# Cross-attention in two layers: an output projection and a later unit's query projection share one slot, and K and V are made in halves in the slots between

## The chip, the cores and the metric

The kernel runs on one core of one Trainium2 chip. Its time is the device time in microseconds (us) of one execution. The median of three runs of the kernel before is 974.39 us (973.72 to 974.40).

The engines by their short names: PE is TensorE (matmuls), and PEld its weight loads; DVE is VectorE; ACT is ScalarE; POOL is GpSimd; SP is SyncE, which only issues DMAs here.

## What is computed

Two cross-attention layers in a row over x, 32 samples of 256 positions by 320 channels, all in fp32. Each sample has a context of 77 rows by 512 channels, the same in both layers. Per layer, with 20 heads of 16 channels:

```python
q = heads(x @ Wq);  k = heads(ctx @ Wk);  v = heads(ctx @ Wv)
p = softmax(q @ k.T / 4)               # over the 77 context rows
x = merge(p @ v) @ Wo + bias + x
```

The reference has more branches (object, "others" and image keys), but the context has exactly the 77 text rows, so the other branches get no rows.

## The kernel before

**Units.** Samples go in 16 pairs. A unit is one pair in one layer, so there are 32 units. Four pairs of layer 0 come first, and then layer 1 of a pair and layer 0 of a later one alternate. Channels lie on the partitions: channels 0 to 255 as two blocks of 128 rows (each 2 samples x 256 columns), and the last 64 channels of both samples together as one block of 128 rows, sample 0 above sample 1 (columns `2*NT:NX`). A *group* g is one such 128 x 256 piece; g = 0 to 3 are the main pieces (channel block g//2, sample g%2), g = 4 is the block of last channels.

**Work of a unit.** Keys and values are projected from the context (`keys`, `keys_rest`, `vals`), queries from x (`queries` for groups 0 to 3, `queries_rest` for group 4). `maxima` computes scores with queries as rows, and DVE takes each row's maximum. `turn` transposes these on DVE, and eight small DMAs write them into spare rows of q. Keys are kept in two masked forms: `kT` for `maxima` (`mask_keys`, POOL) and `kM` for `scores` (`less_keys`, POOL). `scores` computes scores with keys as rows, now less the maximum, and ACT takes the exponentials. `values` multiplies them with V (`products`), then DVE transposes the result (`turned`), takes the reciprocal of the sums, and POOL multiplies (`normal`). `turn_back` transposes it back on DVE into `oT`. `finish` and `finish_rest` are the output projection for groups 0 to 3 and for group 4; `add` (DVE) adds bias and x. `store` writes x out after layer 1. V is made by chunks of 128 context rows, 20 chunks a layer, over the limits of pairs (`load_chunk`, `vals`), and then copied by DMA to the unit that needs it (`place_vals`).

**Tiles on PE.** Every projection is cut into column tiles of 32 output channels (`by_columns`, line 183). A product over 320 input channels has two full steps over 128 rows (`main_channels`) and one over the last 64. For groups 0 to 3 the last 64 channels are taken as 64-row tiles, sample 0 in rows 0 to 63 and sample 1 in rows 64 to 127, in different PSUM banks (`last_channels`, line 196). For group 4 (`project_rest`, line 217) all three steps have 128 rows; the third uses a weight `w22` that is block-diagonal, so that half of its rows are zeros. A matmul in fp32 shows as two records in the profile. Maxima and scores use 32-row tiles.

**PSUM.** One pool of eight banks serves everything; a bank is handed out again in turn, once its reader is done.

**Order.** The program is written in slots, by hand (lines 490 to 569). Unit u begins its scores at slot s = 5u, and there are five slots a unit, each with one group of maxima (of the next unit but one, or the next), one of scores, one of values, and some projection as filler. Within a slot the kinds of work come in the order of line 565: load, maxima, turn, scores, values, rest, back, full, last. `at(slot, where, step)` puts a step in its place. Each engine and each DMA queue then runs its own instructions in this order. Relative to s, before: x loads at s-14, context at s-12, `queries` at s-9 ("last"), `keys` at s-8, `keys_rest` at s-7, `vals` at s-6 (and s-5, where a second chunk is needed), `queries_rest` and `less_keys` at s-5, maxima from s-6 to s-2, `turn` at s-2, scores from s, values and `turn_back` one slot after each, `finish` at s+6 ("full"), `finish_rest` at s+8. So `finish` of one unit and `queries` of the third next stand in the same slot. The last units but one (`late`) have their output projections in parts, over the slots at the end, which have no other filler.

Of the kernel before, what the change touches and what calls it, by code (L numbers as in the profile page):

```python
# [47 lines left out]
F32 = mybir.dt.float32  # L49
# [6 lines left out]
P = 128  # L56
NB = 2
# [33 lines left out]
def xattn_kernel(ctx: ExitStack, tc: tile.TileContext, xT, cT, cP, weights, outT):  # L91
# [104 lines left out]
    def last_channels(ps, w2, x, ts=(0, 1), **flags):  # L196
        for t in ts:
            for b in range(NB):
# [18 lines left out]
    def project_rest(ps, w, w22, x):  # L217

        for kc in range(3):
            for i in range(4):  # L220
                b, m = i // 2, i % 2
                r = slice(32 * i, 32 * i + 32)
                if kc < 2:
                    lhsT = w[:, kc, 2 * P + 32 * m : 2 * P + 32 * m + 32]
                    rhs = x[:, kc * NT + b * S : kc * NT + (b + 1) * S]
                else:
                    lhsT, rhs = w22[:, 0, r], x[:, 2 * NT : NX]
                nc.tensor.matmul(ps[r, 0:S], lhsT, rhs, start=(kc == 0), stop=(kc == 2))  # L228


    def mask_keys(u, g0, g1):

        kR, kT = st[u]["kr"], st[u]["k"]
        engine = nc.gpsimd if u else nc.vector
        for e in range(2):
            engine.tensor_scalar_mul(kT[:, e, g0:g1], kR[:, g0:g1], masks[:, e : e + 1])  # L236
# [10 lines left out]
    def keys(u):  # L247
        p, layer = units[u]
        w, c_sb = w_sb[layer], cs[u]
        kR = st[u]["kr"] = work.tile([P, NG, L], F32, tag="kR", name=f"kR_{u}", bufs=2)  # L250
        st[u]["k"] = work.tile([P, 2, NG, L], F32, tag="kT", name=f"kT_{u}", bufs=3)
        for t in range(2):
            ps = bank(f"psk_{u}_{t}")
            for kc in range(NKA):
                by_columns(
                    ps[:, 0 : 2 * L],
                    w["k"][:, kc, t * P : (t + 1) * P],
                    c_sb[:, kc, :],
                    start=(kc == 0),
                    stop=(kc == NKA - 1),  # L260
                )
            nc.scalar.copy(kR[:, 2 * t : 2 * t + 2].rearrange("p g k -> p (g k)"), ps[:, 0 : 2 * L])  # L262
        mask_keys(u, 0, 4)

    def keys_rest(u):
# [4 lines left out]
        for kc in range(NKA):  # L270
            for i in range(4):
                b, m = i // 2, i % 2
# [8 lines left out]
        mask_keys(u, 4, 5)  # L281

    def queries(u):
        p, layer = units[u]
        w = w_sb[layer]
        q0, _ = st[u]["q"] = [
            work.tile([P, NX], F32, tag=f"q{e}", name=f"q{e}_{u}", bufs=3) for e in range(2)
# [377 lines left out]
```

## Time and profile before

| | |
|---|---|
| median of 3 runs | 974.39 us (973.72 to 974.40) |
| profiled execution, its own time | 974.26 us |
| its span, first to last instruction | 972.5 us |
| granted PE clock | 1.000 |
| PE busy | 965.8 us (99%) |
| DVE, ACT, POOL busy | 567.6 (58%), 430.2 (44%), 238.8 us (25%) |
| one unit in the middle (454.0 to 483.3 us) | 29.3 us |
| its longest slot (481.95 to 493.48: outputs and queries) | 11.53 us |
| its shortest slot (507.38 to 511.30: query rest) | 3.92 us |
| DMA, mean | 86 GB/s |

How to read the lines below. The page's first line gives, for each engine, busy time, share of the span and number of instructions. The chain is the work that ended last, followed back, as shares of the span. A line of waits reads: engine, tile and line, what it waited for, us in total, times, longest. A line of the timeline reads: start in us from the span's begin, length in us, engine, line, operation, output and inputs by tile, tile shape (rows*columns), operand shapes, number of instructions merged; in brackets the idle time before and what ended it. Ends of matmuls are modelled, so the distance from one group's start to the next's is the time that a group took.

### The profile page before, as it was taken

Reading aid. Unit: us, or ns where it says so; the run is one execution under the profiler, and the core shown is the slowest. Engines: PE = TensorE matmul, PEld = TensorE weight load, DVE = VectorE, ACT = ScalarE, POOL = GpSimd, SP = SyncE. Lnnn points to the kernel's source line nnn. Section 1 sums busy time; section 2 is a strip of 40 time slices with the busy share of each in tenths; the row PEclk is TensorE's granted clock in tenths of the full one; section 3 lists DMA queues with packets and bytes.
Section 4 is the critical chain, followed back from the end, with each engine's and each line's share of the span. In section 5 each row is a group of like instructions: output and inputs, shape, how many; then the busy total and the mean of one; then the engine's idle time right before and its main releaser. Section 6 shows DMA issues by size and latency. Waiting matters only on the chain.

```text
span 972.5 us, 43974 instructions
## 1 busy us (share of the span) xinstructions
PE 965.8 (99%) x19674; PEld 597.1 (61%) x19674; DVE 567.6 (58%) x1320; ACT 430.2 (44%) x937; POOL 238.8 (25%) x360
## 2 busy tenths in 40 slices
PE   8999999999999999999999999999999999999998
PEld 5666666666666666665666656666666666566654
DVE  2456555665655665556655556655566555565664
ACT  1445434454444454444544444544445444444543
POOL 2233221332221322212222223222132221232211
PEclk9999999999999999999999999999999999999999
DMA  6632122231132411223112232221322212230112
GB/s 221 238 103 79 46 71 97 71 100 46 55 124 72 135 47 59 97 82 124 56 60 87 70 126 72 73 73 65 126 82 71 69 52 98 71 107 25 49 58 83
DMA packets 54526, 83.60 MB, mean 86 GB/s; under 512 B 15620, under 2 KB 36228, under 8 KB 54338
## 3 DMA queue, kind: packets, MB, share of 16 engines
q1 hardware_dynamic: 53386, 78.29, 24.3%
q8 instruction: 154, 2.52, 1.1%
q10 hardware_dynamic: 952, 2.50, 0.7%
q14 instruction: 34, 0.28, 0.1%
HBM read 35.39 MB, written 10.49 MB: 47 GB/s over the span
## 4 chain that ended last, share of the span: by engine, by line
PE 99%; DVE 1%; POOL 0%; issue 0%; ACT 0%; POOLq 0%
PE po L412 16%; PE psq L186 15%; PE psy L186 15%; PE pss L392 14%; PE psm L357 12%; PE psv L186 9%; PE psk L186 7%; PE psq L228 4%; PE psy L228 4%; PE psk L273 2%; PE warm L179 0%; DVE max L365 0%; DVE kT L236 0%; POOL stage L156 0%; POOL normal L433 0%
## 5 line engine op out<-in xcount | busy, mean ns | idle before, releaser
L398 ACT ACTIVATE pT<-pss 77x512 f32<-77x512 f32 x640 | 327.4, 591 | 209.0 <-PE pss L392 209.0
L365 DVE TENSOR_REDUCE max<-psm 128x4 f32<-128x308 f32 x640 | 260.4, 469 | 179.2 <-PE psm L357 175.5
L433 POOL TENSOR_TENSOR normal<-turned,inv 128x256 f32<-128x256 f32 x160 | 99.5, 622 | 677.6 <-DVE inv L428 677.6
L412 PE MATMUL po<-pT,v 77*32 77x256 f32 x2560 | 171.5, 385 | 0.5 <-DVE max L365 0.5
L392 PE MATMUL pss<-q,kM 32*77 32x256 f32 x2560 | 168.6, 374 | 0.0
L186 PE MATMUL psq<-x,w 128*32 128x256 f32 (+1 forms) x3072 | 150.7, 382 | 0.0
L186 PE MATMUL psy<-oT,w 128*32 128x256 f32 (+1 forms) x3072 | 150.4, 380 | 0.0
L298 ACT COPY q<-psq 128x256 f32<-128x256 f32 x128 | 47.1, 373 | 204.0 <-PE psq L186 195.6
L424 DVE STREAM_TRANSPOSE turned<-po 128x512 f32<-128x512 f32 x160 | 113.4, 709 | 39.0 <-PE po L412 36.0
L447 DVE STREAM_TRANSPOSE oT<-normal 128x256 f32<-128x256 f32 x160 | 71.3, 445 | 108.4 <-POOL normal L433 108.4
L357 PE MATMUL psm<-kT,q 32*128 32x154 f32 x2560 | 129.0, 314 | 0.9 <-DVE kT L236 0.7
L357 PEld LDWEIGHTS psm<-kT,q 32*128 32x128 f32 x2560 | 92.1, 183 | 56.1 <-issue 34.6
L186 PEld LDWEIGHTS psq<-x,w 128*32 128x32 f32 (+1 forms) x3072 | 85.6, 109 | 58.7 <-issue 15.3
L412 PEld LDWEIGHTS po<-pT,v 77*32 77x32 f32 x2560 | 67.0, 109 | 87.8 <-DVE max L365 57.8
L186 PEld LDWEIGHTS psy<-oT,w 128*32 128x32 f32 (+1 forms) x3072 | 81.2, 108 | 63.4 <-issue 15.6
L392 PEld LDWEIGHTS pss<-q,kM 32*77 32x77 f32 x2560 | 102.2, 141 | 17.6 <-issue 1.2
L236 POOL TENSOR_SCALAR kT<-kR,masks 128x308 f32<-128x308 f32 (+1 forms) x124 | 93.9, 769 | 38.6 <-ACT kR L262 32.0
L454 DVE SCALAR_TENSOR_TENSOR x<-psy,w,x 128x256 f32<-128x256 f32 x160 | 68.6, 477 | 56.4 <-PE psy L186 51.3
L186 PE MATMUL psv<-w,cv 128*32 128x320 f32 x1232 | 93.5, 432 | 0.0
L186 PE MATMUL psk<-c,w 128*32 128x154 f32 x2048 | 73.2, 294 | 0.0
L186 PEld LDWEIGHTS psk<-c,w 128*32 128x32 f32 x2048 | 66.0, 110 | 6.7 <-issue 0.4
L186 PEld LDWEIGHTS psv<-w,cv 128*32 128x32 f32 x1232 | 41.1, 110 | 40.6 <-issue 2.2
(28 smaller groups left out, 354.0 us busy)
## 6 DMA issues: line engine op xcount, KB each, us to landing
q<-q SPq DMA_DIRECT2D x32, 640.0 KB
c<-in_cP_dram SPq DMA_DIRECT2D x32, 308.0 KB
cv<-in_cT_dram SPq DMA_DIRECT2D x38, 256.0 KB
out_dram<-x SPq DMA_DIRECT2D x15, 640.0 KB
x<-in_xT_dram SPq DMA_DIRECT2D x14, 640.0 KB
v<-stage SPq DMA_DIRECT2D x26, 192.5 KB
q<-mT SPq DMA_DIRECT2D x254, 5.0 KB
w<-in_w_dram ACTq DMA_DIRECT2D x2, 640.0 KB
```

The costliest lines, as they stand in the source:

```text
L186: nc.tensor.matmul(out[m : m + 32], lhsT[:, m : m + 32], rhs, **flags)
L228: nc.tensor.matmul(ps[r, 0:S], lhsT, rhs, start=(kc == 0), stop=(kc == 2))
L236: engine.tensor_scalar_mul(kT[:, e, g0:g1], kR[:, g0:g1], masks[:, e : e + 1])
L357: nc.tensor.matmul(ps[j][:, c * 2 * L : (c + 1) * 2 * L], q[r, c * P : (c + 1) * P], kT[r, :, g, :], start=True, stop=True,)
L365: nc.vector.tensor_reduce(mx[:, 2 * g : 2 * g + 2, 2 * j : 2 * j + 2], ps[j][:, : 4 * L].rearrange("p (c e k) -> p c e k", e=2, k=L), AX.X ...
L392: nc.tensor.matmul(ps[j][:L, e * S : (e + 1) * S], kM[r, e, g, :], q[r, :], start=True, stop=True,)
L398: nc.scalar.activation(st[u]["p", g][j][:L], ps[j][:L], AF.Exp, scale=SCALE)
L412: nc.tensor.matmul(po[32 * j : 32 * j + 32, e * S : (e + 1) * S], vpad[:L, b, pair, e].rearrange("p a d -> p (a d)"), pT[j][:L, e * S : (e ...
L424: nc.vector.transpose(turned[:, 0 : 2 * S], po)
L433: nc.gpsimd.tensor_tensor(normal.rearrange("p q e d -> p e q d"), outs, inv.unsqueeze(3).broadcast_to([P, 2, S // 32, HD]), ALU.mult,)
L447: nc.vector.transpose(of_group(st[u]["o"], g), normal)
L454: nc.vector.scalar_tensor_tensor(x, ps[:, 0:S], w_sb[layer]["b"][:, 0, t : t + 1], x, ALU.add, ALU.add)
```

## The change

- The output projection of unit u-3 and the query projection of unit u become one step, `outputs_and_queries`, at slot s-10, the rests of both included. It runs for units 3 to 30. Its order on PE: main channels of the outputs, main channels of the output rest, all last channels as 64-row tiles, main channels of the query rest, main channels of the queries. The last channels of the two rests no longer use the zero-padded 128-row step: each is cut by samples into 64-row tiles, and the query rest is laid out with the two samples swapped (`swap`), so that an output rest's tiles and a query rest's take different columns of the array. The layout of group 4 of keys and of the values' output follows that swap.
- That step opens ten PSUM banks: four and one for the outputs, one and four for the queries. The `add`s come behind all 64-row tiles.
- `keys` is made in two halves (slots s-9 and s-8), with `keys_rest` at s-9; `kT` becomes three tiles with a mask pass each. `vals` is made in two halves of 160 columns: at s-7 and s-6 for one new chunk, both halves of a chunk in a slot where there are two.
- Loads, maxima and `turn` come one slot earlier. `turn_back` of groups 0 to 3 moves to the next slot, behind its maxima ("turn back" in the order).
- The late units' parts are moved by one slot or more; `queries` and `queries_rest` stay separate for units 1, 2 and 31.

```diff
-    def last_channels(ps, w2, x, ts=(0, 1), **flags):
+    def last_channels(ps, w2, x, ts=(0, 1), bs=(0, 1), **flags):
...
-    def project_rest(ps, w, w22, x):
-        for kc in range(3):
+    def rest_tile(ps, i, lhsT, rhs, swap, **flags):
+        o = (32 * i + 64 * swap) % P
+        nc.tensor.matmul(ps[o : o + 32, 0:S], lhsT, rhs, **flags)
+    def rest_main(ps, w, x, start, stop, swap=0):
+        for kc in range(2):
             for i in range(4):
                 b, m = i // 2, i % 2
-                r = slice(32 * i, 32 * i + 32)
-                if kc < 2:
-                    lhsT = w[:, kc, 2 * P + 32 * m : 2 * P + 32 * m + 32]
-                    rhs = x[:, kc * NT + b * S : kc * NT + (b + 1) * S]
-                else:
-                    lhsT, rhs = w22[:, 0, r], x[:, 2 * NT : NX]
-                nc.tensor.matmul(ps[r, 0:S], lhsT, rhs, start=(kc == 0), stop=(kc == 2))
-    def mask_keys(u, g0, g1):
-        kR, kT = st[u]["kr"], st[u]["k"]
+                rest_tile(
+                    ps, i, w[:, kc, 2 * P + 32 * m : 2 * P + 32 * m + 32],
+                    x[:, kc * NT + b * S : kc * NT + (b + 1) * S], swap,
+                    start=(start and kc == 0), stop=(stop and kc == 1),
+                )
+    def rest_last(ps, w22, x, b, swap=0, **flags):
+        r = slice(64 * b, 64 * b + 64)
+        for i in (2 * b, 2 * b + 1):
+            rest_tile(ps, i, w22[r, 0, 32 * i : 32 * i + 32], x[r, 2 * NT : NX], swap, **flags)
...
+    def project_rest(ps, w, w22, x, swap=0):
+        rest_main(ps, w, x, start=True, stop=False, swap=swap)
+        for i in range(4):
+            rest_tile(
+                ps, i, w22[:, 0, 32 * i : 32 * i + 32], x[:, 2 * NT : NX], swap,
+                start=False, stop=True,
+            )
+    def mask_keys(u, t):
+        kR, groups = st[u]["kr"], slice(2 * t, min(2 * t + 2, NG))
+        n = groups.stop - groups.start
+        kT = work.tile([P, 2, n, L], F32, tag=f"kT{t}", name=f"kT_{u}_{t}", bufs=2)
+        st[u]["k", t] = kT
         engine = nc.gpsimd if u else nc.vector
         for e in range(2):
-            engine.tensor_scalar_mul(kT[:, e, g0:g1], kR[:, g0:g1], masks[:, e : e + 1])
+            engine.tensor_scalar_mul(kT[:, e], kR[:, groups], masks[:, e : e + 1])
     def less_keys(u):
...
-    def keys(u):
+    def keys(u, t):
         p, layer = units[u]
         w, c_sb = w_sb[layer], cs[u]
...
+        nc.scalar.copy(kR[:, 2 * t : 2 * t + 2].rearrange("p g k -> p (g k)"), ps[:, 0 : 2 * L])
+        mask_keys(u, t)
     def keys_rest(u):
...
         for kc in range(NKA):
             for i in range(4):
-                b, m = i // 2, i % 2
+                b, m = 1 - i // 2, i % 2
...
         nc.scalar.copy(st[u]["kr"][:, 4], ps[:, 0:L])
-        mask_keys(u, 4, 5)
+        mask_keys(u, 2)
+    def new_queries(u):
+        st[u]["q"] = [
+            work.tile([P, NX], F32, tag=f"q{e}", name=f"q{e}_{u}", bufs=3) for e in range(2)
+        ]
+        return st[u]["q"][0]
...
-        project_rest(ps, w["q"], w["q22"], xs[p])
+        project_rest(ps, w["q"], w["q22"], xs[p], swap=1)
         nc.scalar.copy(of_group(q0, 4), ps[:, 0:S])
         nc.sync.dma_start(out=q1, in_=q0)
-        less_keys(u)
+    def outputs_and_queries(u, uq):
+        w, wq, o, x = w_sb[units[u][1]], w_sb[units[uq][1]], st[u]["o"], xs[units[uq][0]]
+        q0 = new_queries(uq)
+        y = [[bank(f"psy_{u}_{t}_{b}") for b in range(NB)] for t in range(2)]
+        main_channels(y, w["o"], o, start=True, stop=False)
+        y2 = bank(f"psy_{u}_2")
+        rest_main(y2, w["o"], o, start=True, stop=False)
+        q2 = bank(f"psq_{uq}_2")
+        q = [[bank(f"psq_{uq}_{t}_{b}") for b in range(NB)] for t in range(2)]
+        def rests(b):
+            rest_last(y2, w["o22"], o, b, start=False, stop=True)
+            rest_last(q2, wq["q22"], x, b, swap=1, start=True, stop=False)
+        def outputs(t, b):
+            last_channels(y, w["o2"], o, (t,), (b,), start=False, stop=True)
+        outputs(0, 0), rests(1)
+        outputs(1, 0), outputs(0, 1)
+        rests(0), outputs(1, 1)
+        last_channels(q, wq["q2"], x, start=True, stop=False)
+        for g in range(4):
+            add(u, g, y[g // 2][g % 2])
+        add(u, 4, y2)
+        store(u)
+        rest_main(q2, wq["q"], x, start=False, stop=True, swap=1)
+        nc.scalar.copy(of_group(q0, 4), q2[:, 0:S])
+        main_channels(q, wq["q"], x, start=False, stop=True)
+        for g in range(4):
+            nc.scalar.copy(of_group(q0, g), q[g // 2][g % 2][:, 0:S])
+        nc.sync.dma_start(out=st[uq]["q"][1], in_=q0)
...
-    def vals(layer, i):
+    def vals(layer, i, h):
         n = min(P, B * L - i * P)
-        stage, c_sb = stages[layer][i % 2], cvs.pop((layer, i))
-        ps = bank(f"psv_{layer}_{i}")
+        stage, c_sb = stages[layer][i % 2], cvs[layer, i]
+        ps = bank(f"psv_{layer}_{i}_{h}")
...
+        cols, pairs = slice(h * C // 2, (h + 1) * C // 2), slice(5 * h, 5 * h + 5)
         for kc in range(NKA):
             by_columns(
-                ps[:n, :C],
+                ps[:n, : C // 2],
                 c_sb[:, kc, :n],
-                w_sb[layer]["v"][:, kc, :],
+                w_sb[layer]["v"][:, kc, cols],
...
         nc.scalar.copy(
-            stage[:n].rearrange("p r e a d -> p r (e a) d")[:, :, 0:4:3, :],
-            ps[:n, :C].rearrange("p (r e d) -> p r e d", e=2, d=HD),
+            stage[:n, pairs].rearrange("p r e a d -> p r (e a) d")[:, :, 0:4:3, :],
+            ps[:n, : C // 2].rearrange("p (r e d) -> p r e d", e=2, d=HD),
         )
...
-                    kT[r, :, g, :],
+                    kT[r, :, g % 2, :],
...
         for e in range(2):
             for j in range(4):
                 if g < 4:
-                    b, pair = g % 2, 4 * (g // 2) + j
+                    b, pair, o = g % 2, 4 * (g // 2) + j, 32 * j
                 else:
-                    b, pair = j // 2, 8 + j % 2
+                    b, pair, o = 1 - j // 2, 8 + j % 2, (32 * j + 64) % P
...
-        if u not in late:
-            store(u)
...
     late = {
-        NU - 4: (end - 9, end - 8, end - 12),
+        NU - 4: (end - 10, end - 9, end - 8),
         NU - 3: (end - 7, end - 6, end - 5),
         NU - 2: (end - 4, end - 1, end - 3),
     }
...
     for u, (p, layer) in enumerate(units):
         s = NG * u
         if layer == 0 and u > 0:
-            at(s - 14, "load", lambda p=p: load_x(p))
+            at(s - 15, "load", lambda p=p: load_x(p))
         if u > 0:
-            at(s - 12, "load", lambda u=u: load_context(u))
+            at(s - 13, "load", lambda u=u: load_context(u))
         if u > 1:
-            at(s - 8, "rest", lambda u=u: keys(u))
-            at(s - 9, "last", lambda u=u: queries(u))
-            at(s - 7, "rest", lambda u=u: keys_rest(u))
+            at(s - 9, "rest", lambda u=u: keys(u, 0))
+            at(s - 9, "rest", lambda u=u: keys_rest(u))
...
+            at(s - 8, "rest", lambda u=u: keys(u, 1))
+        paired = u > 2 and u - 3 not in late
+        if paired:
+            at(s - 10, "full", lambda u=u: outputs_and_queries(u - 3, u))
+        else:
+            if u > 1:
+                at(s - 10, "last", lambda u=u: queries(u))
+            at(s - 6, "rest", lambda u=u: queries_rest(u))
+        at(s - 6, "rest", lambda u=u: less_keys(u))
         need = range(p * NB * L // P, ((p + 1) * NB * L - 1) // P + 1)
-        when = s - 6
+        new = [i for i in need if i >= made[layer]]
+        made[layer] += len(new)
+        slots = {}
+        for k, i in enumerate(new):
+            at(s - 10 + k, "load", lambda layer=layer, i=i: load_chunk(layer, i))
+            for h in range(2):
+                slots[i] = s - 7 + (k if len(new) > 1 else h)
+                at(slots[i], "full", lambda layer=layer, i=i, h=h: vals(layer, i, h))
         for i in need:
-            if i < made[layer]:
-                at(when, "full", lambda u=u, i=i: place_vals(u, i))
-                continue
-            at(when - 3, "load", lambda layer=layer, i=i: load_chunk(layer, i))
-            at(when, "full", lambda layer=layer, i=i: vals(layer, i))
-            at(when, "full", lambda u=u, i=i: place_vals(u, i))
-            made[layer] += 1
-            when = s - 5
-        at(s - 5, "rest", lambda u=u: queries_rest(u))
+            at(slots.get(i, s - 7), "full", lambda u=u, i=i: place_vals(u, i))
         for g in range(NG):
             if u > 0:
-                at(s - 6 + g, "maxima", lambda u=u, g=g: maxima(u, g))
+                at(s - 7 + g, "maxima", lambda u=u, g=g: maxima(u, g))
             at(s + g, "scores", lambda u=u, g=g: scores(u, g))
             at(s + g + 1, "values", lambda u=u, g=g: values(u, g))
-            at(s + g + 1, "back", lambda u=u, g=g: turn_back(u, g))
+            if g < 4:
+                at(s + g + 2, "turn back", lambda u=u, g=g: turn_back(u, g))
+            else:
+                at(s + g + 1, "back", lambda u=u, g=g: turn_back(u, g))
         if u > 0:
-            at(s - 2, "turn", lambda u=u: turn(u))
+            at(s - 3, "turn", lambda u=u: turn(u))
         if u == NU - 1:
...
-            continue
-        at(late[u][2] if u in late else s + NG + 3, "rest", lambda u=u: finish_rest(u))
-        if u not in late:
-            at(s + NG + 1, "full", lambda u=u: finish(u))
-            continue
...
     at(3, "load", lambda: load_weights(1, "v", "v", nc.sync))
     at(4, "load", lambda: load_weights(1, "o", "b", nc.sync))
-    order = ("load", "maxima", "turn", "scores", "values", "rest", "back", "full", "last")
+    order = (
+        "load", "maxima", "turn", "turn back", "scores", "values", "rest", "back", "full", "last",
+    )
...
```

More of the change, by code (lines that the diff above doesn't have):

```diff
@@ L192, in of_group @@
         return x[:, 2 * NT : NX]
-    def last_channels(ps, w2, x, ts=(0, 1), **flags):
+    def last_channels(ps, w2, x, ts=(0, 1), bs=(0, 1), **flags):
         for t in ts:
-            for b in range(NB):
+            for b in bs:
                 r = slice(64 * b, 64 * b + 64)
@@ L245, in less_keys @@
             )
-    def keys(u):
+    def keys(u, t):
         p, layer = units[u]
         w, c_sb = w_sb[layer], cs[u]
[L250 to L263, printed above, removed]
+        if t == 0:
+            st[u]["kr"] = work.tile([P, NG, L], F32, tag="kR", name=f"kR_{u}", bufs=2)
+        kR = st[u]["kr"]
+        ps = bank(f"psk_{u}_{t}")
+        for kc in range(NKA):
+            by_columns(
+                ps[:, 0 : 2 * L],
+                w["k"][:, kc, t * P : (t + 1) * P],
+                c_sb[:, kc, :],
+                start=(kc == 0),
+                stop=(kc == NKA - 1),
+            )
+        nc.scalar.copy(kR[:, 2 * t : 2 * t + 2].rearrange("p g k -> p (g k)"), ps[:, 0 : 2 * L])
+        mask_keys(u, t)
     def keys_rest(u):
@@ L285, in queries @@
         w = w_sb[layer]
-        q0, _ = st[u]["q"] = [
-            work.tile([P, NX], F32, tag=f"q{e}", name=f"q{e}_{u}", bufs=3) for e in range(2)
-        ]
+        q0 = new_queries(u)
         ps = [[bank(f"psq_{u}_{t}_{b}") for b in range(NB)] for t in range(2)]
@@ L350, in maxima @@
     def maxima(u, g):
-        q0, kT, mx = st[u]["q"][0], st[u]["k"], maxes[u % 2]
+        q0, kT, mx = st[u]["q"][0], st[u]["k", g // 2], maxes[u % 2]
         q = of_group(q0, g)
@@ L408, in products @@
                 if g < 4:
-                    b, pair = g % 2, 4 * (g // 2) + j
+                    b, pair, o = g % 2, 4 * (g // 2) + j, 32 * j
                 else:
-                    b, pair = j // 2, 8 + j % 2
+                    b, pair, o = 1 - j // 2, 8 + j % 2, (32 * j + 64) % P
                 nc.tensor.matmul(
-                    po[32 * j : 32 * j + 32, e * S : (e + 1) * S],
+                    po[o : o + 32, e * S : (e + 1) * S],
                     vpad[:L, b, pair, e].rearrange("p a d -> p (a d)"),
@@ L536, in xattn_kernel @@
             at(s + NG, "last", lambda u=u: finish_rest(u))
-            continue
-        at(late[u][2] if u in late else s + NG + 3, "rest", lambda u=u: finish_rest(u))
-        if u not in late:
-            at(s + NG + 1, "full", lambda u=u: finish(u))
-            continue
-        for t in range(2):
-            at(late[u][t], "full", lambda u=u, t=t: finish(u, (t,)))
-        at(max(late[u]), "last", lambda u=u: store(u))
-    at(-10, "last", lambda: queries(0))
-    at(-9, "rest", lambda: keys(0))
-    at(-9, "rest", lambda: keys_rest(0))
+        if u in late:
+            for t in range(2):
+                at(late[u][t], "full", lambda u=u, t=t: finish(u, (t,)))
+            at(late[u][2], "rest", lambda u=u: finish_rest(u))
+            at(max(late[u]), "last", lambda u=u: store(u))
+    at(-10, "last", lambda: queries(0))
+    for u, slot in ((0, -9), (1, -4)):
+        for t in range(2):
+            at(slot, "rest", lambda u=u, t=t: keys(u, t))
+        at(slot, "rest", lambda u=u: keys_rest(u))
     for slot, g in ((-6, 0), (-5, 1), (-4, 2), (-4, 3), (-3, 4)):
@@ L552, in xattn_kernel @@
     at(-3, "turn", lambda: turn(0))
-    at(-4, "rest", lambda: keys(1))
-    at(-4, "rest", lambda: keys_rest(1))
     at(-3, "last", lambda: queries(1))
@@ L563, in xattn_kernel @@
     at(4, "load", lambda: load_weights(1, "o", "b", nc.sync))
-    order = ("load", "maxima", "turn", "scores", "values", "rest", "back", "full", "last")
+    order = (
+        "load", "maxima", "turn", "turn back", "scores", "values", "rest", "back", "full", "last",
+    )
     for slot in range(min(s for s, _ in place), max(s for s, _ in place) + 1):
```

## The prediction

> **What bounds the kernel now.** I read the page's busy line and its chain first, then what TensorE (PE) waited for, then PE's timeline over one unit, then the groups by shape.
>
> ```profile
> PE 965.8 (99%) x19674; PEld 597.1 (61%) x19674; DVE 567.6 (58%) x1320; ACT 430.2 (44%) x937; POOL 238.8 (25%) x360
> ...
> PE 99%; DVE 1%; POOL 0%; issue 0%; ACT 0%; POOLq 0%
> ```
>
> ```profile
> PE warm L179 <- POOL ident masks.py:199: 1.9, 1, 1.9
> PE psm L357 <- DVE kT L236: 0.7, 1, 0.7
> PE po L412 <- DVE max L365: 0.5, 1, 0.5
> PE psm L357 <- issue: 0.3, 1, 0.3
> ```
>
> The chain that ended last is PE from end to end, and PE waited 3.4 us in all, at the start. A PE that is called busy could still run slowly, so the next view is the one that counts: when each group of matmuls starts.
>
> ```profile
> 481.95 0.81 PE L357 MATMUL psm<-kT,q 32*128 32x154 f32 x16
> 482.58 1.04 PE L392 MATMUL pss<-q,kM 32*77 32x256 f32 x16
> 483.55 1.07 PE L412 MATMUL po<-pT,v 77*32 77x256 f32 x16
> 484.44 4.66 PE L186 MATMUL psy<-oT,w 128*32 128x256 f32 x96
> 488.89 4.66 PE L186 MATMUL psq<-x,w 64*32 64x256 f32 x96
> 493.48 0.81 PE L357 MATMUL psm<-kT,q 32*128 32x154 f32 x16
> ...
> 495.97 2.29 PE L186 MATMUL psk<-c,w 128*32 128x154 f32 x64
> 498.19 0.81 PE L357 MATMUL psm<-kT,q 32*128 32x154 f32 x16
> ...
> 500.68 1.48 PE L228 MATMUL psy<-oT,w 128*32 128x256 f32 x24
> 501.97 0.72 PE L273 MATMUL psk<-c,w 128*32 128x77 f32 x32
> ...
> 505.11 2.34 PE L186 MATMUL psv<-w,cv 128*32 128x320 f32 x32
> 507.38 0.81 PE L357 MATMUL psm<-kT,q 32*128 32x154 f32 x16
> ...
> 509.89 1.48 PE L228 MATMUL psq<-x,w 128*32 128x256 f32 x24
> 511.30 0.81 PE L357 MATMUL psm<-kT,q 32*128 32x154 f32 x16
> ```
>
> From start to start, a rest (24 records) takes 1.29 us (500.68 to 501.97) when the next group has the same tile shape, and 1.41 us (509.89 to 511.30) when it hasn't. Four column tiles run abreast, so 24 records are 6 steps: **0.216 us a step of 256 columns**, and **0.12 us a change of tile shape**. The output projection checks this: 484.44 to 488.89 is 4.45; 64 records of 128 rows are 16 steps, 3.45, a change 0.12, which leaves 0.88 for 32 records of 64 rows: 4 steps, so *eight* of those run abreast. A V chunk (32 records of 320 columns) is 2.27, 8 steps of 0.269 and a change. K (64 records of 154 columns) is 2.22, 16 steps of 0.131. The last three step times lie on a line: 0.00083 us a column and 0.003 us a step. So PE's time is a count of steps and changes. The other engines matter only where they hold a bank or an input that PE wants; the same stretch of all engines shows when they let go:
>
> ```profile
> 482.96 1.60 DVE L365 TENSOR_REDUCE max<-psm 128x4 f32<-128x308 f32 x4
> ...
> 483.70 2.05 ACT L398 ACTIVATE pT<-pss 77x512 f32<-77x512 f32 x4 [1.24 <-PE pss L392]
> ...
> 488.71 1.66 DVE L454 SCALAR_TENSOR_TENSOR x<-psy,w,x 128x256 f32<-128x256 f32 x4 [1.76 <-PE psy L186]
> ...
> 493.19 0.80 ACT L298 COPY q<-psq 128x256 f32<-128x256 f32 x2 [0.92 <-PE psq L186]
> ```
>
> **The change part by part.**
>
> *1. The rests.* Before, an output rest and a query rest are 6 steps each, 2 of which (128 rows, half of them zeros) hold the last channels: 4 steps. After, those are eight 64-row tiles by two passes: 16 records, eight abreast, 2 steps. The two rests cost 10 steps instead of 12: −2 × 0.216 = −0.432 us. It happens for units 3 to 30 (unit 31's partner is one of the late three): 28 × −0.432 = **−12.1 us**. Changes of shape per unit: the pair slot keeps its three (128 to 64, 64 to 128, 128 to 32 rows), the other four slots keep one each behind their filler. No difference.
>
> *2. V in halves.* 40 chunks, 8 steps of 320 columns each become 16 of 160: 320 steps more at 0.003 us each, **+0.8 us**. K's matmuls are the same ones, spread over two slots. The Trainium skill speaks against this part: TensorEngine Tiling (Array Packing), section Instruction Overhead, gives each matmul about 60 cycles of overhead; 1232 more records at 25 ns (an estimate from that page) would be +31 us, and the whole change some 19 us slower. The rows don't show it: the 154-column step costs what the line through 256 and 320 columns says.
>
> *3. ScalarE (ACT).* One copy more per chunk: 0.43 us at 320 columns becomes two of about 0.30 (between 0.29 at 154 and 0.37 at 256). ACT is 44% busy. In a slot the four exponentials end 3.8 us after the slot's first matmul (483.70 + 2.05 − 481.95), a filler's copy at 4.1. The next scores take that copy's bank (eight banks, handed out in turn) at the slot's length + 0.63. The shortest new slot: 2.49 (481.95 to 484.44) + half of V or K, 8 steps of 0.131 to 0.136, + 0.12 = 3.66 to 3.70, so 4.29. Cover 0.19 us. Cost nothing; without the cover about 0.1 us in each of 3 slots, 28 units: +8.
>
> *4. GpSimd (POOL).* The key masks are six instructions, not four: 2 × 1.05 us at 308 columns become 4 × about 0.68 (between 0.49 at 77 and 1.05 at 308): +0.6 us per unit on an engine that is 25% busy. The keys now come two slots before their maxima. Nothing.
>
> *5. VectorE (DVE), turn_back a slot later.* The transpose of groups 0 to 3 moves behind the next slot's maxima; DVE no longer idles 0.80 us for POOL in front of it. DVE's order decides when banks come free. Tightest is the slot with the turn of the maxima (3.66 us): four maxima of 0.41 from 0.82 (499.01 after 498.19) to 2.45, turn 0.51, oT 0.45, turned 0.72: the bank of po is free at 4.13; the next scores want it at 4.29. Cover 0.16 us, and 0.2 before the next maxima could be read. Cost taken: nothing. If it slips: 0.1 to 0.2 us × 28, +3 to +6. Group 3's transpose ends 3.0 us into the pair slot, its first reader (step 7 of the outputs) comes at 3.8; group 4's at about 5.2 against 6.9.
>
> *6. Ten banks in a pool of eight.* In the pair slot the last two query banks are those of the first two output banks, so PE now waits for DVE's adds in the middle of the slot; behind this wait stand all the query matmuls. The 64-row block starts at T. Output bank 0 is complete after 2 steps, bank 1 after 4. By the row of the adds (first start 488.71, four in 1.66, 0.48 each; T was 488.00) the first add runs T+0.71 to T+1.19; the second starts when bank 1 is done, T+1.16, and ends T+1.64. PE wants bank 1 at step 9, T+1.75. Cover 0.1 us. A release shows about 0.05 us behind its cause (query copies end at 493.99, the weight load behind them starts at 494.04), so it is on the edge: between 0 and 0.15 us × 28 = 0 to +4.2. I take 0.01 each, **+0.3**, since the weight load has a step of lead and the row nearest to it, scores waiting for the last query copy in the pair slot of before, loses nothing.
>
> *7. SyncE's (SP) queue.* Moved one slot earlier: the loads of x, context and chunk, the turn's eight DMAs; the store and q0-to-q1 copy now lie in the pair slot, behind its adds and copies, 0.39 and 0.55 us of issue. The turn's DMAs (4.72 us of issue) start at 3.0 in their slot and end at 7.8; the scores that read them come at 11.7 instead of 9.8. SP issues some 10 us of each 29. Nothing.
>
> *8. Start and tail.* The first V goes ahead of the first maxima, whose wait for the masks (0.67) it may fill; but x of pair 1 now goes ahead of the V weights in ACT's queue, and DMA is saturated until 14 us (371 GB/s from 12 to 14, 29 after), when V would start: 0. The wait of 0.5 us at 55 (DVE behind POOL) should go: −0.8 with what PE loses around it. Three maxima in a row now need 12 banks of 8, and DVE's reductions (8 took 3.17) give them at 0.41 each: up to +1.2. Sum −1.5 to +1.5; I take **+0.2**. The last unit's chain is unchanged.
>
> **Sum.** −12.1 + 0.8 + 0.3 + 0.2 = −10.8 us. The profiled execution took 974.26 us (span 972.5), 0.13 below the median of 974.39. 974.26 − 10.8 = **963.5 us**.
>
> **The rivals.**
>
> *Short slots.* The gain is there, but banks come late (parts 3, 5, 6): the pair slot's wait at 0.15 and the turn slot's at 0.15 take 8.4 of it. For it: DVE would be 97% busy in the turn slot (3.56 of 3.66). Against it: before, a slot of 3.92 us had room, and a bank that came 0.13 us ahead of the scores cost nothing. It gives 966 to 972.
>
> *Slower: the mixed tiles don't run abreast.* The trace shows eight abreast where four tiles of one bank alternate with four of another. Now a group of eight has four in an output bank and two each in both rests' banks. If the six blocks of outputs and rests went one after another, 6 steps would be 12: +1.30 us × 28 = +36, so 974.3 − 10.8 + 36 = 1000 us. It decides from 2 lost steps a unit on. Against it: the eight tiles are still eight different places of the array, and the rests in the trace ran two halves on different data at the full rate. On the page just named, Gotcha 1 (PSUM Pressure) says that different row tiles must not write one bank at once; the order of the blocks keeps to that, and no run here shows a breach.
>
> *No gain.* Something other than PE's steps sets the slots. The unit's 29.3 us are used up by steps and changes to 0.1 us, so there is little room. 974 ± 2.
>
> **How the numbers follow.** The sum holds: 0.70 (own range 961.5 to 966). Short slots: 0.18, all faster. Slower: 0.07. No gain: 0.05, of which 0.03 within 0.2% (1.9 us, about what this measurement can tell) and 0.01 on each side. Faster 0.89, same 0.03, slower 0.08. The range leaves out the slower cases and the upper part of the short slots: 961 to 969.
>
> **What would show it.** Pair slots: 11.53 + 10 steps (the 12 that move in, less 2), 13.7 us; the others 4.2, 3.7, 3.7, 3.7; the unit 28.9 instead of 29.3. The line of the 64-row rests should have 448 records (28 × 16), and the 128-row rests shrink accordingly. Part 6 is wrong if PE's weight load of psq waits for DVE's add of x by more than 0.1 us; part 5 if weight loads of pss wait for DVE's turned; the slower rival shows in a 64-row block of over 2.4 us (10 steps are 2.16, a change 0.12). The prediction fails upward if such waits pass 0.2 us a unit, and downward only if the start gains more than 1.5 us.

## The result

The changed kernel takes 963.41 us (median of 4 runs, 962.88 to 964.23); beside it the kernel before took 974.39 us (973.72 to 974.41). The ratio is 0.989, with a 95% interval of 0.9873 to 0.9907. The profiled execution of the changed kernel took 962.88 us, its span is 961.1 us and the granted PE clock is 1.0. The forecast was 963.5 us.

The page of the changed kernel: busy time, share of the span and instructions of each engine, and the shares of the chain that ended last.

```profile
PE 955.1 (99%) x20906; PEld 629.1 (65%) x20906; DVE 552.9 (58%) x1322; ACT 436.6 (45%) x977; POOL 254.9 (27%) x422
...
PE 98%; DMA 1%; ACTq 0%; issue 0%; DVE 0%
```

PE is still the chain (98%), with 1232 more records and 10.7 us less busy time. So the new records are not what costs; the steps are. What PE waited for in the changed kernel (total us, times, longest):

```profile
PE warm L181 <- POOL ident masks.py:199: 1.9, 1, 1.9
PE psv L188 <- DMA w<-in_w_dram: 0.4, 1, 0.4
PE psq L188 <- issue: 0.2, 1, 0.2
```

All three are single waits at the start. In the 28 units of the middle the profile shows no wait of PE. PE's timeline over one such unit of the changed kernel (start, length, group; the lines left out in the second gap are further groups of the same 64-row block):

```profile
503.58 0.81 PE L421 MATMUL psm<-kT,q 32*128 32x154 f32 x16
...
506.07 3.64 PE L188 MATMUL psy<-oT,w 128*32 128x256 f32 x64
509.53 1.05 PE L222 MATMUL psy<-oT,w 128*32 128x256 f32 x16
510.50 0.42 PE L188 MATMUL psy<-oT,w 64*32 64x256 f32 x4
510.53 0.41 PE L222 MATMUL psy<-oT,w 64*32 64x256 f32 x2
510.54 0.41 PE L222 MATMUL psq<-x,w 64*32 64x256 f32 x2
...
511.82 1.07 PE L188 MATMUL psq<-x,w 64*32 64x256 f32 x32
512.82 1.07 PE L222 MATMUL psq<-x,w 128*32 128x256 f32 x16
513.71 3.64 PE L188 MATMUL psq<-x,w 128*32 128x256 f32 x64
517.28 0.81 PE L421 MATMUL psm<-kT,q 32*128 32x154 f32 x16
...
521.47 0.81 PE L421 MATMUL psm<-kT,q 32*128 32x154 f32 x16
...
525.12 0.81 PE L421 MATMUL psm<-kT,q 32*128 32x154 f32 x16
...
528.82 0.81 PE L421 MATMUL psm<-kT,q 32*128 32x154 f32 x16
...
532.51 0.68 PE L421 MATMUL psm<-kT,q 32*128 32x154 f32 x12
```

The six starts of psm give five slots: 13.70, 4.19, 3.65, 3.70 and 3.69 us, a unit of 28.93. At 510.50 to 510.54 four output tiles, two of the output rest and two of the query rest start within 0.04 us: the mixed block of eight runs abreast. The 64-row block, the queries' last channels included, lasts 2.32 us (510.50 to 512.82); 10 steps of 0.216 and one change of shape are 2.28.

### The profile page after: what moved, and what is told of

Same layout as the page of the kernel before. It is cut to its first block, busy times and chain, and to the rows that moved or that the text cites. A ratio compares the mean times of both kernels' runs of the same rounds, so it can differ in the third digit from the quotient of the medians.

```text
span 961.1 us, 46519 instructions
## 1 busy us (share of the span) xinstructions
PE 955.1 (99%) x20906; PEld 629.1 (65%) x20906; DVE 552.9 (58%) x1322; ACT 436.6 (45%) x977; POOL 254.9 (27%) x422
## 4 chain that ended last, share of the span: by engine, by line
PE 98%; DMA 1%; ACTq 0%; issue 0%; DVE 0%
PE po L476 17%; PE psy L188 15%; PE pss L456 15%; PE psq L188 14%; PE psm L421 12%; PE psv L188 9%; PE psk L188 7%; PE psy L222 4%; PE psq L222 4%; PE psk L296 2%; DMA w<-in_w_dram 1%; ACTq L144 0%; DVE x L518 0%
## 5 line engine op out<-in xcount | busy, mean ns | idle before, releaser
L188 PE MATMUL psy<-oT,w 128*32 128x256 f32 (+1 forms) x3072 | 164.4, 379 | 0.0
L188 PEld LDWEIGHTS psy<-oT,w 128*32 128x32 f32 (+1 forms) x3072 | 88.3, 108 | 63.5 <-issue 16.1
L259 POOL TENSOR_SCALAR kT<-kR,masks 128x154 f32<-128x154 f32 (+1 forms) x186 | 111.4, 614 | 10.6 <-ACT kR L285 10.6
L456 PEld LDWEIGHTS pss<-q,kM 32*77 32x77 f32 x2560 | 98.8, 141 | 19.9 <-issue 1.2
L188 PE MATMUL psv<-w,cv 128*32 128x160 f32 x2464 | 99.2, 299 | 0.4 <-DMA w<-in_w_dram 0.4
L367 ACT COPY q<-psq 128x256 f32<-128x256 f32 x28 | 10.4, 372 | 184.4 <-PE psq L222 184.4
L188 PEld LDWEIGHTS psv<-w,cv 128*32 128x32 f32 x2464 | 82.6, 110 | 15.3 <-PE psk L296 0.6
L511 DVE STREAM_TRANSPOSE oT<-normal 128x256 f32<-128x256 f32 x160 | 68.8, 430 | 26.2 <-POOL normal L497 26.1
L188 PE MATMUL psk<-c,w 128*32 128x154 f32 x2048 | 78.8, 294 | 0.0
```

Source lines behind the costliest of these rows:

```text
L188: nc.tensor.matmul(out[m : m + 32], lhsT[:, m : m + 32], rhs, **flags)
L259: engine.tensor_scalar_mul(kT[:, e], kR[:, groups], masks[:, e : e + 1])
L456: nc.tensor.matmul(ps[j][:L, e * S : (e + 1) * S], kM[r, e, g, :], q[r, :], start=True, stop=True,)
L511: nc.vector.transpose(of_group(st[u]["o"], g), normal)
```

## The experiments

Each is an edit of the changed kernel. All of them compute the whole reference; the third has a spare instruction more.

**1. The rests padded again.** The ten banks, the slot order and the halves stay; only the rests' last channels go back to the zero-padded 128-row step.

```diff
-        rest_main(y2, w["o"], o, start=True, stop=False)
+        project_rest(y2, w["o"], w["o22"], o)
...
-        outputs(0, 0), rests(1)
-        outputs(1, 0), outputs(0, 1)
-        rests(0), outputs(1, 1)
+        outputs(0, 0), outputs(0, 1)
+        outputs(1, 0), outputs(1, 1)
...
-        rest_main(q2, wq["q"], x, start=False, stop=True, swap=1)
+        project_rest(q2, wq["q"], wq["q22"], x, swap=1)
```

> The kernel after, but both rests take their last channels again as one zero-padded step of 128 rows (two steps each); everything else, the slots, the halves of K and V and the order, stays. Count of steps: two steps more in each of 28 pair slots, 28 x 0.432 = +12.1 us, 975.5 us, and a pair slot of 14.13 instead of 13.70 us. Rival (the gain comes from the new order: fewer waits of DVE for POOL, earlier loads): 963 to 966 us.

Measured: 975.48 us (974.81 to 977.48), ratio to the kernel before 1.0015 (1.0006 to 1.0024). PE's timeline of this kernel over its pair slot:

```profile
510.59 0.81 PE L416 MATMUL psm<-kT,q 32*128 32x154 f32 x16
...
516.54 1.48 PE L222 MATMUL psy<-oT,w 128*32 128x256 f32 x24
...
519.83 1.50 PE L222 MATMUL psq<-x,w 128*32 128x256 f32 x24
...
524.72 0.81 PE L416 MATMUL psm<-kT,q 32*128 32x154 f32 x16
```

Each rest has its 24 records again, and the slot is 14.13 us instead of 13.70: 0.43, the two steps. 975.48 − 963.41 = 12.07 us is more than the whole gain; all the rest of the change costs 1.2 us against the kernel before, which took 974.26 us beside this run (0.6 to 2.3 by the ratio's interval), where the prediction had 1.3. None of it lies in the middle: from the scores of one unit to those of the next, a unit with one new V chunk takes 29.36 us in this kernel, 29.36 in the kernel before and 28.93 in the changed one.

**2. Blocks of the same rows next to each other.** The order of the six blocks was made so that neighbours use different halves of the array's rows. Here the two output blocks on the upper rows come first, then three blocks on the lower rows.

```diff
-        outputs(0, 0), rests(1)
-        outputs(1, 0), outputs(0, 1)
-        rests(0), outputs(1, 1)
+        outputs(0, 0), outputs(1, 0)
+        rests(1), outputs(0, 1)
+        outputs(1, 1), rests(0)
```

> The kernel after, but the six blocks of last channels of outputs and rests stand in another order: the output blocks of the upper rows, then the blocks of the lower rows, then one of each, so that twice two blocks of the same rows follow each other. If tiles run abreast only with the neighbours in the order: 8 steps instead of 6, 28 x 0.432 = +12.1, 975.5 us. Rival (PE finds the free half of the array by itself, whatever the order): 963.4 us, no change.

Measured: 969.17 us (969.0 to 969.6), ratio 0.995 (0.9935 to 0.9965): 5.8 us more than the changed kernel, which neither theory gave. Divided by 28 it is 0.21 us, one step a unit. PE's timeline of this kernel shows why it is not two:

```profile
514.25 0.42 PE L188 MATMUL psy<-oT,w 64*32 64x256 f32 x4
514.31 0.41 PE L222 MATMUL psy<-oT,w 64*32 64x256 f32 x2
...
514.71 0.67 PE L188 MATMUL psy<-oT,w 64*32 64x256 f32 x16
...
516.78 1.07 PE L222 MATMUL psq<-x,w 128*32 128x256 f32 x16
```

In the program `outputs(1, 0)` stands before `rests(1)`. But the rests' records (L222, at 514.31) start 0.06 us behind the first output block, whose eight records start at 514.25 and 514.49, and the first record of `outputs(1, 0)` starts at 514.71. So PE filled the free rows with a block that stands behind another one, and only one step was lost: the 64-row part is 2.53 us (514.25 to 516.78) instead of 2.32.

**3. DVE's second add later.** One more DVE instruction between the first and the second add tests how near the edge the last query banks are.

```diff
+    spare = const.tile([P, 2, S], F32, name="spare")
+    nc.vector.memset(spare, 0.0)
...
             add(u, g, y[g // 2][g % 2])
+            if g == 0:
+                nc.vector.transpose(spare[:, 1], spare[:, 0])
```

> The kernel after, with one more DVE instruction (a transpose of 128x256 of a spare tile, 0.37 to 0.45 us) between the first and the second add, so that the bank of the last query block comes free that much later. If the cover was on the edge (0.1 us or less): a loss of 0.2 to 0.35 us in each of 28 pair slots, +6 to +10, 969 to 973 us. Rival (the release has room to spare): 963.4, no change.

Measured: 969.22 us (968.91 to 969.47), ratio 0.9949 (0.9935 to 0.9964): +5.8 us, 0.21 a unit. Lines of both engines in the timeline of this kernel:

```profile
514.44 0.48 DVE L522 SCALAR_TENSOR_TENSOR x<-psy,w,x 128x256 f32<-128x256 f32 x1 [2.63 <-PE psy L190]
514.84 0.43 DVE L366 STREAM_TRANSPOSE spare<-spare 128x256 f32<-128x256 f32 x1
515.05 1.28 PE L190 MATMUL psq<-x,w 64*32 64x256 f32 x32
515.20 1.62 DVE L522 SCALAR_TENSOR_TENSOR x<-psy,w,x 128x256 f32<-128x256 f32 x4
516.26 1.07 PE L224 MATMUL psq<-x,w 128*32 128x256 f32 x16
```

The 64-row queries take 1.21 us (515.05 to 516.26) instead of 1.00 (511.82 to 512.82). The single records make the edge exact; times are from the block's start. In the changed kernel the second add ends at 1.69, the weight loads of the bank it frees start at 1.74, and the matmuls of that step start at 1.75 and after, in the same rhythm of 0.216 as the ones before. In this run the add ends at 1.91, the loads start at 1.96, and one step is lost. From the end of the add to the load are 0.05 us in both runs, in each of the 28 units. So the edge is where the prediction had it, nearly: the second add ends at 1.69 and not at 1.64, and the changed kernel is on the good side by some hundredths of a us, since its load starts 0.01 us ahead of the step's first matmul (1.74 and 1.75) and 0.04 ahead of the first one on its own rows. The loads for the other half of the rows of that step start 0.2 us ahead of it.

**4. `turn_back` where it was before.** Groups 0 to 3 are turned back in the slot of their values again.

```diff
-            if g < 4:
-                at(s + g + 2, "turn back", lambda u=u, g=g: turn_back(u, g))
-            else:
-                at(s + g + 1, "back", lambda u=u, g=g: turn_back(u, g))
+            at(s + g + 1, "back", lambda u=u, g=g: turn_back(u, g))
```

> The kernel after, but turn_back of groups 0 to 3 stands in the slot of its values again, where DVE waits 0.8 us for POOL in front of it. If the new short slots stand on DVE's order: the maxima of the next slot start 0.7 us late behind the turn's slot and about 0.4 us late behind the other two of 3.7 us, and the products wait for the first of them: about 0.43 + 0.1 + 0.1 us a unit, +12 to +20 us, 975 to 983 us. Rival (PE's steps alone set the slots): 963.4, no change.

Measured: 977.59 us (976.98 to 978.8), ratio 1.0035 (1.0022 to 1.0048): 14.2 us more, which eats the whole gain. One line of DVE's waits in this kernel, and then PE's timeline over the scores and values in the slot with the turn and in the next:

```profile
DVE oT L511 <- POOL normal L497: 125.9, 157, 0.8
```

```profile
534.84 1.04 PE L456 MATMUL pss<-q,kM 32*77 32x256 f32 x16
536.11 1.07 PE L476 MATMUL po<-pT,v 77*32 77x256 f32 x16 [0.23 <-DVE max L429]
...
538.84 1.04 PE L456 MATMUL pss<-q,kM 32*77 32x256 f32 x16
539.92 1.07 PE L476 MATMUL po<-pT,v 77*32 77x256 f32 x16
```

DVE idles 0.8 us for POOL in nearly every slot (125.9 us in 157 waits; the changed kernel's line has 26.1 in 33). In slots of 3.7 us that no longer fits: PE gets po's bank late, 1.27 us after the scores' start instead of 0.97, and 0.11 late in each of the next two slots. That is 0.52 us in this unit and would be 14.6 us over 28. In the changed kernel part 5 costs nothing, but without it the short slots do.

**5. V of a chunk whole.** A chunk is made in one slot, and with one new chunk a unit (24 chunks of 40) the next slot has no filler.

```diff
-            for h in range(2):
-                slots[i] = s - 7 + (k if len(new) > 1 else h)
-                at(slots[i], "full", lambda layer=layer, i=i, h=h: vals(layer, i, h))
+            slots[i] = s - 7 + k
+            at(slots[i], "full", lambda layer=layer, i=i: vals(layer, i))
```

> The kernel after, but a V chunk is one piece of 320 columns again, in the slot where its first half was; a unit with one new chunk (24 of 32) then has no filler in the next slot, which PE could do in 2.6 us. By PE's steps alone (rival): 320 steps of 0.003 us less, -0.8, 962.6 us. If a short slot is held up by banks: the scores behind it want the bank of the last exponential, which ends at 3.8 us into the slot, at 3.1: about +0.75 us x 24, less 0.8, +12 to +18 us, 975 to 981 us.

Measured: 976.65 us (975.57 to 978.25), ratio 1.0024 (1.0012 to 1.0035): +13.2 us, although the kernel has fewer records. Its PE timeline at the slot without filler:

```profile
507.59 0.81 PE L420 MATMUL psm<-kT,q 32*128 32x154 f32 x16
...
510.22 0.81 PE L420 MATMUL psm<-kT,q 32*128 32x154 f32 x16
510.85 1.67 PE L455 MATMUL pss<-q,kM 32*77 32x256 f32 x16
512.45 1.07 PE L475 MATMUL po<-pT,v 77*32 77x256 f32 x16
```

The slot takes 2.63 us (507.59 to 510.22), less than ACT's and DVE's share of a slot, and the next scores pay: 1.60 us to po instead of 0.97. PE shows no wait here, because its 16 scores are spread over 1.67 us instead of 1.04. The waits are at the weight loads. The loads of these scores that start at 510.95 and 511.43 follow 0.05 us behind the ends of two of ACT's exponentials, at 510.90 and 511.38. In this profile the loads of scores wait 5.8 us for ACT's exponentials, in 21 waits, and in the changed kernel they have no such line. So the scores wait for the banks that ACT frees late, as the expectation had it.

**6. V in quarters.** The price of a step, by more and shorter ones: 80 columns instead of 160.

```diff
-        for kc in range(NKA):
-            by_columns(
-                ps[:n, : C // 2],
...
+        for part in range(2):
+            c0 = part * C // 4
+            for kc in range(NKA):
+                by_columns(
+                    ps[:n, c0 : c0 + C // 4],
...
```

> The kernel after, but V is made in quarters of 80 columns, two behind each other into one bank with one copy as before: 640 more steps of half the length, 2464 more records. By the line through the steps of 154, 256 and 320 columns: 0.003 us a step more, +1.9 us, 965.3 us. Rival, the 60 cycles per matmul of the Trainium skill's page TensorEngine Tiling (Array Packing), an estimate of 25 ns for each record more: +62 us, 1025 us.

Measured: 972.69 us (971.61 to 975.24), ratio 0.9987 (0.9979 to 0.9996): +9.3 us, and neither theory had that. The price of a step itself came out as the rows had it: in a slot with half a chunk, V takes 1.222 us from start to start instead of 1.202 with 8 more steps, 0.0025 each, so 640 steps are 1.6 us. Most of the other 7.7 stand in a kind of wait that the changed kernel has only once (0.2 us). PE's waits of the quarters kernel that ended in issue, with psq's 0.6 (once) left out:

```profile
PE psv L188 <- issue: 3.7, 5, 1.1
...
PE psm L423 <- issue: 0.9, 2, 0.5
```

And its timeline in a slot with two half chunks:

```profile
122.84 2.11 PE L188 MATMUL psv<-w,cv 128*32 128x80 f32 x108
125.71 0.61 PE L188 MATMUL psv<-w,cv 128*32 128x80 f32 x20 [0.76 <-issue]
```

PE stops in the middle of a block, for nothing that another engine or a DMA of the program does. The profile has eight such pauses, 5.2 us of idle time; counted from the last start before a pause to the first behind it, which needs no modelled end, they are 7.3 us. The next two runs ask where this comes from.

**7 and 8. Quarters only where a unit makes one chunk, and only where it makes two.** In the first, a slot has at most 64 V records; in the second, quarters lie in the slots with two half chunks, 128 records in 2.2 us. The edit of the first; the second has `parts = 2 if len(new) > 1 else 1`.

```diff
-                at(slots[i], "full", lambda layer=layer, i=i, h=h: vals(layer, i, h))
+                parts = 1 if len(new) > 1 else 2
+                at(slots[i], "full", lambda layer=layer, i=i, h=h, parts=parts: vals(layer, i, h, parts))
```

> V in quarters of 80 columns, but only in the units that make one chunk of V (24 of 40 chunks; the other 16, which lie two to a unit, stay in halves). 24 x 16 more steps at the 0.0025 us that the V slots of the quarters run showed are +1.0 us: 964.4 if the other 8 us of the quarters run come only where a slot holds over 100 short records in a row (the slots with two half chunks, and the start). If they come with every added record, wherever it is, 24 of 40 parts of +9.3 are +5.6: 969.0. In the first case the line of V (psv) shows next to no idle time that ended in issue.

> The other part: V in quarters only in the units that make two chunks (16 of 40 chunks). If the loss comes where a slot holds over 100 short records in a row: 16 x 16 x 0.0025 = 0.6 for the steps and about 7.7 for the waits, 971.7. If it comes with every added record: 16 of 40 parts of +9.3, +3.7, 967.1. The waits that ended in issue should stand at the first V of the slots with two half chunks, as in the quarters run, 0.5 to 1.1 us each.

Measured: one chunk, 964.96 us (964.25 to 965.25), ratio 0.9905 (0.989 to 0.992): +1.55. Two chunks, 970.09 us (969.21 to 970.42), ratio 0.9955 (0.9943 to 0.9968): +6.7, for 1024 added records instead of 1440. So the loss does not go with the number of records; it goes with where they are dense. Each of these two-chunk slots takes 2.33 us for its 128 V records and a change of shape where nothing stops it. Of the 16 in a kernel, 6 in the quarters kernel and 5 in the two-chunk kernel take longer, by 0.35 to 1.9 us; the one-chunk kernel has no pause that ended in issue. The two-chunk kernel shows the idle time again; its timeline in one of the slots with two half chunks:

```profile
889.63 2.39 PE L188 MATMUL psv<-w,cv 128*32 128x80 f32 x126
892.97 0.30 PE L188 MATMUL psv<-w,cv 128*32 128x80 f32 x2 [0.95 <-issue]
```

The trace also has the packets of a queue that brings instructions, 16 KB each. That these are PE's is read from their number: 164 in the changed kernel and 183 in the quarters kernel, 19 more for 2464 PE records more, some 130 records a packet. Set against PE's idle stretches that ended in issue (us from the span's start):

```
kernel        packet landed   PE goes on   difference
quarters          14.14         15.55         1.41
quarters         124.15        125.71         1.56
quarters         356.89        358.21         1.32
quarters         746.01        747.38         1.37
two chunks        22.05         23.62         1.57
two chunks       360.69        362.00         1.31
two chunks       654.27        655.53         1.26
two chunks       891.61        892.97         1.36
```

Of 14 such stretches over 0.2 us in the two kernels, 13 end 1.2 to 1.6 us behind a packet's landing, a window that covers 7.5% of the time (183 packets x 0.4 us in 971.5); the other ends 3.3 us behind one. The changed kernel's one wait of this kind, at 31.04, ends 1.5 behind one too. Two packets never follow each other by less than 3.25 us, in the changed kernel or in these. 128 records in 2.2 us is faster than that, so a dense slot lives on what came ahead of it, and whether that lasts differs from slot to slot. So PE seems to run out of instructions: that dense slots pause is shown by the two runs, and the cause is read from the times; no run changed the queue itself.

**9. The start mended.** The second group of maxima goes a slot earlier, so that not three stand in a row, and x of pair 1 is loaded one slot later, behind the V weights.

```diff
-    for slot, g in ((-6, 0), (-5, 1), (-4, 2), (-4, 3), (-3, 4)):
+    for slot, g in ((-6, 0), (-6, 1), (-4, 2), (-4, 3), (-3, 4)):
...
-            at(s - 15, "load", lambda p=p: load_x(p))
+            at(s - 14 if p == 1 else s - 15, "load", lambda p=p: load_x(p))
```

> The kernel after, with two changes of the start alone: the second group of maxima of unit 0 goes one slot ahead, in front of the query rest and the second V chunk, so that three groups no longer follow each other; x of pair 1 is loaded one slot later, behind the V weights. If the start is on PE's chain: -1.2 (the three groups take 3.24 us for 2.0 of steps) and up to -0.4 (the wait for the V weights), 961.8 to 962.3 us. Rival (something else sets the end of the start, such as the turn's DMAs): 963.4.

Measured: 961.87 us (960.83 to 961.95), ratio 0.9869 (0.9854 to 0.9884): 1.5 us less than the changed kernel, and the fastest of all that ran. The maxima at the start, in the changed kernel's timeline and then in this one's:

```profile
20.48 3.31 PE L421 MATMUL psm<-kT,q 32*128 32x154 f32 x48
23.71 2.31 PE L188 MATMUL psk<-c,w 128*32 128x154 f32 x64
```

```profile
16.47 1.34 PE L421 MATMUL psm<-kT,q 32*128 32x154 f32 x32
17.90 1.50 PE L222 MATMUL psq<-x,w 128*32 128x256 f32 x24
...
21.50 1.34 PE L421 MATMUL psm<-kT,q 32*128 32x154 f32 x32
22.87 2.31 PE L188 MATMUL psk<-c,w 128*32 128x154 f32 x64
```

Three groups took 3.23 us; at 0.63 us a group (503.58 to 504.21) and a change they would be 2.0. Two groups take 1.43 and 1.37, where 1.38 is due, so the stall of 1.2 us is gone. The spans of the two profiled executions differ by as much, 961.1 and 959.9 us. What the later load of x gives was not run by itself: the wait for the V weights is gone in this profile, and one of 0.2 us that ended in issue stands there instead.

## Why the prediction was right, step by step

The likeliest case came about, and the mechanism was the one forecast. That the median came within 0.1 us of the forecast is luck in part. Against the profiled execution the sum was −10.8 us; measured there, 974.26 to 962.88, it is −11.4, and this execution of the changed kernel was 0.5 us faster than the median. Inside the sum two errors nearly cancel. A middle unit with one V chunk went from 29.357 to 28.927 us, −0.430, which is 12.0 over 28, where parts 1, 2 and 6 together had −11.0. The start and the end then cost about 0.6, where 0.2 was taken.

*Part 1, the rests.* Right: −12.1 predicted, 12.07 between the changed kernel and the padded one (the kernel before moved by 0.13 between the two measurements); slots 13.70 and 14.13. The trace's line of 64-row rests has the 448 records (2 x 224). The slower rival's condition, mixed tiles not abreast, is refuted by the first 0.04 us of the block. The run with the other order shows that its price was too high as well: six blocks in a bad order don't go one after another, since PE takes the free rows where it can.

*Part 2, V in halves.* Right in size. Two halves behind each other take 2.29 us from start to start (349.70 to 351.99 in the changed kernel), a whole chunk 2.27 (505.11 to 507.38 before): 0.02 for 8 steps more, 0.8 to 0.9 us over 40 chunks. The quarters gave 0.0025 us a step. The part's own product was slightly off, since 320 × 0.003 is 0.96 and not 0.8. In the unit this price does not show: the first scores of a unit, which took 1.00 us to the values before (508.01 to 509.01), take 0.97 now, and these 0.03 us, which the sum did not have, make up for V's.

The Trainium skill's page TensorEngine Tiling (Array Packing), section Instruction Overhead, gives each matmul about 60 cycles of overhead. Added to every record, as the prediction's counter-estimate had it, this would have made the change slower. The measurement decides, and it differs from that reading: 8 steps (32 records) more cost 0.02 us. The same section says that a matmul of one column takes as long as one of 60, which would be a floor; no run here has tiles so narrow.

What the step law lacks is a bound: at 128 records in 2.2 us another limit shows. The change stays under it: its halves have 64 records in such a slot.

*Parts 3 and 5, ACT's copies and `turn_back`.* Right at 0 for the change as it stands: no wait of PE for ACT or DVE in the middle, and slots of 3.65 to 3.70 us as forecast. In the turn's slot DVE frees the bank of po at 525.40, 0.35 us ahead of the next scores (525.75), where the prediction had a cover of 0.16. How little room there is shows in the experiments with `turn_back` as before (+14.2) and V whole (+13.2). The rival of short slots had the right mechanism; the price it named, 8.4 us and up to the range's end at 972, is lower than either of these. It did not come about, because every slot has its half of a filler and DVE no longer waits for POOL in front of the transposes of groups 0 to 3.

*Parts 4 and 7, POOL and SP.* In the changed kernel PE waits for neither in the middle, and DVE's wait for POOL before `oT` fell from 108.4 to 26.1 us in all, which is part 5's doing. Nothing more was tested.

*Part 6, ten banks.* Right, and on the edge as said: +0.3 taken, nothing measurable lost. The second add ends 0.05 us later than worked out (1.69 for 1.64), because it starts behind the first add and not when bank 1 is done. A second add 0.22 us later still costs one whole step, 0.21 us a unit, so the upper end of 0.15 was somewhat low.

*Part 8, the start.* Inside its range of −1.5 to +1.5, but not at the value taken: about +0.6 with the end, for +0.2. Up to +1.2 was given for three maxima in a row, and all of it came (3.23 instead of 2.0 us). The first V was put at 0; in the changed kernel's profile it waits 0.4 us for the V weights, and in the profile with `turn_back` as before, whose start is the same, 2.0. The wait of 0.5 us at 55 is gone, as expected. `queries` of unit 2, at 39.30, takes 5.07 us instead of 4.62 (40.26 to 44.88 before), which the prediction did not have. The trace says why: the weight loads of its 64-row part wait for banks that DVE's maxima still hold, two of them 0.23 us each, and start 0.05 us behind the ends of these maxima (39.82 behind 39.77, 40.21 behind 40.16).

## What to carry to other kernels

On a kernel that PE bounds, count steps and changes of shape from start to start in the timeline; a saving of steps holds fully only if every other engine still fits into the shortened slot, so the filler has to be spread and the waits inside other engines' chains have to go in the same change. Where a bank is handed on in the middle of a slot, set the end of its reader against the step that wants it, in hundredths of a us: being late by a little costs a whole step. Before cutting matmuls shorter, look at how many records a short stretch then holds, since the supply of instructions has a rate of its own.

## What the runs showed of the hardware that was not expected

- PE starts records of a later block on free rows while an earlier block of the program waits for its own rows: the rests at 514.31, the block before them in the program at 514.71. The wrong order cost 0.21 us a unit and not 0.43.
- Instructions arrive in packets of 16 KB, some 130 PE records each, never closer than 3.25 us. Where 128 V records stand in 2.2 us, 6 and 5 of 16 such slots were stretched. PE idles for 0.2 to 1.6 us at a time and goes on 1.2 to 1.6 us after the next packet has landed (13 of 14 pauses).
- Between the end of the add that frees a bank and the weight load that waits for it are 0.05 us. The step is kept with that load 0.01 us ahead of the step's first matmul; an add that ends 0.22 us later costs exactly one step.
